# One exponent shift per query block instead of one per head pair, in an attention kernel

## The chip, the cores and the metric

The kernel runs on one core of one Trainium2 chip. The metric is the device time of one execution in microseconds (us), lower is better. The kernel before took 1887.35 us, the median of three runs (1886.14 to 1888.05).

## What is computed

A cross-attention layer with a residual, followed by a small recurrent (state-space) layer. `x` is 4096 x 512 (four sequences of 1024), the context is 3202 x 512, there are 8 heads of 64. All of it is fp32.

```python
def _mha(q_in, kv_in, W_qkv, b_qkv, W_o, b_o):
    ...
    q, k, v = (heads(q_in, Wq, bq), heads(kv_in, Wk, bk), heads(kv_in, Wv, bv))
    scores = jnp.einsum('bhqd,bhkd->bhqk', q, k) * (1.0 / np.sqrt(HD))
    attn = jax.nn.softmax(scores, axis=-1)
    out = jnp.einsum('bhqk,bhkd->bhqd', attn, v)
    ...
x = residual + _mha(_layernorm(x, g1, beta1), _layernorm(ctx, g1, beta1), ...)
xn = _layernorm(x, g2, beta2)
U = (xn @ W_in.T + b_in) @ Bmat
def step(s, u_t):
    s = jax.nn.silu(s @ A.T) + u_t
    return (s, s)
_, states = jax.lax.scan(step, ...)
x = x + states @ Cmat
return x + mod[:, None, :]
```

A softmax is the same whatever number is subtracted from all the scores of a row ahead of the exponential. The number need only keep the exponentials in range, so it may come from a sample of the keys.

## The kernel before

**Tiling.** The queries form 8 blocks Q of 512. The 3202 keys are 25 chunks of 128 and two left-over keys. The eight heads are four pairs hp; a pair fills 128 partitions, 64 for each head. A *unit* is one block and one head pair, with 25 key steps; block 7 is cut into halves (8 units of 13 steps). TensorE (PE) works on four pieces of 64x64 of its array at a time here, so that two heads and two halves of a chunk run beside each other.

**One step.** `scores` (PE, L1166) makes the scores of a chunk; `weights` (ScalarE, ACT, L1265) takes their exponential with the bias `shift`; `product` (PE, L1327) multiplies by the values; `add` (VectorE, DVE, L1273) adds the weights to `acc`, whose sum over partitions is the denominator. After the last step `fold`, `swap` (an ACT copy that exchanges the partition halves), `gather` (DVE), `sums` (PE) and `den` finish the unit.

**The shift.** Ahead of each unit (in block 7 of each first half), 32 times in all, a sample of 62 keys and the two left-over ones is scored: `sample` (PE, L1198, tile `sm` <- `q`, `kx`), `maximum` (DVE, L1212, L1213), `spread` (PE, L1220, a product that brings each partition's maximum to all of them), `base` (DVE, L1233, L1234, tile `shifts`). The left-over keys' weights come from the same scores: `extra` (ACT, L1240) takes their exponential, `rest` (two DVE operations on two rows, L1250) adds them to `acc`, and products with `vx` (L1316, L1340) add their values.

**Order.** Each engine runs its instructions in the order in which they are written, and waits for what the next one needs. The class `Plan` sets that order. Every piece of work has an engine, a cost, the pieces that it comes after, the buffers that it takes and gives, and a due time. `order()` plays the engines through time, and each free engine takes the ready piece with the earliest due time. The table `SHIFT` adds to the due time of each sort of piece its entry times a step of 2150 ns.

```python
due += self.SHIFT.get(sort, 0) * STEP
```

**Stages.** There are two plans. The first is the *lead* (`lead()`): context chunks c are loaded (`cx_c`), normalized (`xh_c`), turned by PE (`tp_c`, L347), copied to `ct`, and multiplied into keys and values. In the lead, chunks go in groups of four, g = 0 to 6. Group 0's values are plain products (`pv_c`, L619); groups 1 to 5 use seven products in place of eight on quarter tiles (L406): banks `pkx`, `pky`, `pvx`, `pvy` of a group take products of `ct_g`, of the sums `t5_g` and `t7_g` (made by DVE, L812) and of the weights' sums `sk5`, `sk7`, `sv5`, `sv7`. Joins (DVE, L602: `ks_2_22 <- pky_2` and so on) empty these banks. Of a group from 1 on, some chunks reach `ct_g` by DVE transposes (`pair_g`, L501) and 16 small transfers issued by SyncE (SP, L513). The last pieces of the lead are the query products of block 0 (`pq_0_hp`, L376), of which it has three. The second plan is the main one: all units, and between their steps the queries of the next block (seven products, L406, 128x128 tiles), the output projections and the recurrent part, whose last sweeps (L2051, L2125) form the tail. Both plans allow a buffer kind only as many open uses as its ring has.

## Time and profile before

| | |
|---|---|
| median of three runs | 1887.35 us |
| the profiled execution | 1886.87 us |
| its span, first to last instruction | 1885.1 us |
| TensorE busy in the span | 1871.5 us (99%) |
| VectorE busy | 1530.4 us (81%) |
| ScalarE busy | 1145.0 us (61%) |
| GpSimd (POOL) busy | 291.7 us (15%) |
| mean granted TensorE clock | 0.998 of full speed |

The profile comes from one execution. A row of its groups gives line, engine, operation, output tile <- input tiles, tile shape, number of records, then busy time in us and the mean ns of one record, then the idle time before and what ended it. One fp32 product leaves two records. A row of the timeline gives the start, the time from the first start to the last end of a run of like instructions (such runs overlap with the next), engine, line, operation and count; in brackets the idle time before it and what ended it. SPq and ACTq are the issuing of transfers by those engines. The lead ends at 195.3 us, and the tail begins at about 1780.

### The profile page before, as it was taken

To read this page: it belongs to the slowest core of one execution; us is meant where nothing else is said; L and a number is where in the kernel's file an instruction comes from. 1 tells how busy PE (TensorE), PEld (TensorE's weight loads), DVE (VectorE), ACT (ScalarE), POOL (GpSimd) and SP (SyncE) were. 2 spreads that over 40 slices of the span, in tenths; PEclk is the share of its full clock that TensorE was granted. 3 is DMA by queue.
4 is the path that set the end of the run, shared out by engine and by line. 5 is a ranking of instruction groups with operands and counts; after the bars stand their busy time and mean duration, and the time that the engine had idled before them with its cause. 6 is when DMAs were issued, how large, how long until landed. Compare 5 with 4: busy or idle time off the path is not lost.

```text
span 1885.1 us, 45215 instructions
## 1 busy us (share of the span) xinstructions
PE 1871.5 (99%) x18208; PEld 1027.5 (55%) x18208; DVE 1530.4 (81%) x1918; ACT 1145.0 (61%) x1439; POOL 291.7 (15%) x386
## 2 busy tenths in 40 slices
PE   9999999999999999999999999999999999999997
PEld 5887356545453535444454545353544545677674
DVE  6642689698888979798979888898979897998776
ACT  3242677565756567675656575657657565757653
POOL 6120300023000230023002200013002300101105
PEclk9999999999999999999999999999999999999999
DMA  8552242222333234313432233322431333435577
GB/s 256 162 168 88 63 121 75 90 65 80 107 98 105 68 86 122 100 45 93 109 107 68 76 104 99 106 68 88 125 93 44 91 102 92 151 105 162 158 200 233
DMA packets 260674, 206.04 MB, mean 109 GB/s; under 512 B 94633, under 2 KB 233897, under 8 KB 260461
## 3 DMA queue, kind: packets, MB, share of 16 engines
q1 hardware_dynamic: 256440, 196.48, 36.2%
q10 hardware_dynamic: 4020, 6.62, 1.2%
q8 instruction: 146, 2.39, 0.5%
q14 instruction: 68, 0.55, 0.1%
HBM read 156.32 MB, written 29.88 MB: 99 GB/s over the span
## 4 chain that ended last, share of the span: by engine, by line
PE 98%; DVE 1%; ACT 1%; DMA 0%; issue 0%; POOL 0%; SPq 0%; ACTq 0%; DVEq 0%; POOLq 0%
PE po L1327 33%; PE s L1166 32%; PE po L1352 5%; PE s L1179 4%; PE pax L406 3%; PE qx L406 3%; PE pay L406 2%; PE qy L406 2%; PE pkx L406 2%; PE pvx L406 2%; PE pvy L406 1%; PE pky L406 1%; PE pk L742 1%; PE pv L619 1%; PE sm L1198 1%; PE pu L1838 1%
## 5 line engine op out<-in xcount | busy, mean ns | idle before, releaser
L1265 ACT ACTIVATE p<-s,shifts 128x1024 f32<-128x1024 f32 x804 | 886.9, 1109 | 458.2 <-PE s L1166 336.4
L1273 DVE TENSOR_TENSOR acc<-p,acc 128x1024 f32<-128x1024 f32 (+1 forms) x732 | 894.8, 1225 | 119.0 <-ACT p L1265 90.8
L1327 PE MATMUL po<-p,v 64*64 64x512 f32 x5600 | 804.1, 590 | 0.0
L1166 PE MATMUL s<-q,k 64*64 64x512 f32 x5600 | 802.0, 589 | 0.0
L1166 PEld LDWEIGHTS s<-q,k 64*64 64x64 f32 x5600 | 263.6, 133 | 343.9 <-issue 291.2
L1327 PEld LDWEIGHTS po<-p,v 64*64 64x64 f32 x5600 | 264.7, 133 | 300.0 <-issue 260.1
L1725 POOL TENSOR_TENSOR xr<-xr,rowb 128x512 f32<-128x512 f32 x28 | 35.6, 1271 | 783.0 <-DVE acc L1273 570.5
L1439 DVE RECIPROCAL rd<-rd 128x256 f32<-128x256 f32 (+1 forms) x64 | 110.1, 1721 | 3.4 <-ACT rd L1434 3.1
L1179 PE MATMUL s<-q,k 64*64 64x256 f32 x1600 | 109.4, 378 | 0.2 <-ACT p L1265 0.2
L1352 PE MATMUL po<-p,v 64*64 64x256 f32 x1600 | 107.5, 377 | 0.0
L1820 POOL TENSOR_TENSOR xr<-x,modb 128x512 f32<-128x512 f32 x28 | 35.5, 1275 | 291.2 <-DVE acc L1273 238.3
L1179 PEld LDWEIGHTS s<-q,k 64*64 64x64 f32 x1600 | 67.3, 133 | 24.1 <-issue 4.9
L1352 PEld LDWEIGHTS po<-p,v 64*64 64x64 f32 x1600 | 67.8, 133 | 16.9 <-issue 0.5
L1296 ACT COPY swap<-acc 64x512 f32<-64x512 f32 (+1 forms) x70 | 40.2, 574 | 41.9 <-DVE acc L1273 40.2
L1212 DVE TENSOR_REDUCE m<-sm 128x1 f32<-128x256 f32 x64 | 24.0, 417 | 41.2 <-PE sm L1198 41.2
L1273 DVE TENSOR_TENSOR acc<-p,p 128x1024 f32<-128x1024 f32 x36 | 44.0, 1222 | 14.5 <-ACT p L1265 14.5
L1506 POOL TENSOR_SCALAR rstd_x<-mv_x 128x1 f32<-128x1 f32 x28 | 18.2, 648 | 231.3 <-DVE mv_x L1503 227.0
L602 DVE TENSOR_TENSOR ks<-pky,ks 128x512 f32<-128x512 f32 x15 | 10.4, 691 | 43.6 <-PE pky L406 22.2
L1301 DVE TENSOR_TENSOR acc<-swap,acc 64x512 f32<-64x512 f32 (+1 forms) x70 | 44.1, 630 | 1.5 <-ACT swap L1296 0.2
L1656 ACT ACTIVATE q<-qx,bias 128x256 f32<-128x256 f32 x42 | 17.6, 470 | 45.3 <-PE qx L406 45.3
L596 ACT ACTIVATE ks<-pkx,bias 128x256 f32<-128x256 f32 x40 | 16.8, 470 | 43.7 <-PE pkx L406 31.1
L1250 DVE TENSOR_TENSOR acc<-x,acc 2x512 f32<-2x512 f32 x56 | 38.0, 678 | 0.7
(321 smaller groups left out, 1849.0 us busy)
## 6 DMA issues: line engine op xcount, KB each, us to landing
k<-kd SPq DMA_DIRECT2D x432, 128.0 KB, 2.3
v<-vd SPq DMA_DIRECT2D x432, 128.0 KB, 2.4
xn<-x SPq DMA_DIRECT2D x448, 32.0 KB, 1.9
xr<-in_x_dram SPq DMA_DIRECT2D x30, 256.0 KB, 3.6
x1d<-xr SPq DMA_DIRECT2D x30, 256.0 KB, 3.1
x<-in_x_dram SPq DMA_DIRECT2D x28, 256.0 KB, 3.2
cx<-in_ctx_dram SPq DMA_DIRECT2D x25, 256.0 KB, 4.9
kd<-ks SPq DMA_DIRECT2D x20, 256.0 KB, 2.5
```

The source lines that it names most:

```text
L406: nc.tensor.matmul(to[:, b, :], still[:, i, b * P : (b + 1) * P], moving[:, i, :], start=(start and b == 0 and i == 0), stop=(i == 1), ski ...
L1166: nc.tensor.matmul(s[k0 : k0 + HD, a].rearrange("p b j -> p (b j)"), kts[(*w["at"][:2], c // 2)][r, b * CK + k0 : b * CK + k0 + HD], q[r], ...
L1179: nc.tensor.matmul(s[k0 : k0 + HD, a, b, :], kts[(*w["at"][:2], c)][r, b * CK + k0 : b * CK + k0 + HD], q[r], start=True, stop=True, skip_ ...
L1250: made = nc.vector.tensor_tensor(to[r], t[r], to[r], ALU.add)
L1265: nc.scalar.activation(t[:, :, :nb, :], w["ps"][c][:, :, :nb, :], AF.Exp, bias=w["shift"])
L1273: return nc.vector.tensor_tensor(w["acc"][:, :, :nb, :], t[:, :, :nb, :], before[:, :, :nb, :], ALU.add)
L1296: nc.scalar.copy(w["swap"][r], of[(1 - k) * HD : (2 - k) * HD])
L1301: made = nc.vector.tensor_tensor(of[r], w["swap"][r], of[r], ALU.add)
L1327: nc.tensor.matmul(w["po"][k][a * HD : (a + 1) * HD], vts[Q, hp, c // 2][r, c % 2, a * HD : (a + 1) * HD], t[r, a].rearrange("p b j -> p ( ...
L1352: nc.tensor.matmul(w["po"][k][a * HD : (a + 1) * HD, :QU], vts[Q, hp, c][r, b, a * HD : (a + 1) * HD], t[r, a, b, :], start=(c == 0 and b ...
L1439: nc.vector.reciprocal(w["rd"][:, part], (w["pd"] if last else w["rd"])[:, part])
L1725: return nc.gpsimd.tensor_tensor(xs[half][:, t], xs[half][:, t], rowb, ALU.add)
```

## The change

There is one sample for each block, eight in place of 32, and it covers all four head pairs with 32 keys each (30 and the two left-over ones). `sampled_by(Q)` writes it as seven pieces:

- `sample`: 16 products on 64x32 pieces of the array (32 keys, 256 queries), into two banks;
- `held` (ACT): the two banks are copied to an SBUF tile `ex`;
- `maximum` (DVE): one reduction of 128 x 1024 to 128 x 2;
- `sent`, `got` (SP): 128 x 2 numbers to DRAM, and 256 numbers back to all partitions;
- `base` (DVE): two reductions, then two small operations with the constant `marks`, which pick each partition's own bias for `extra`;
- `extra` (ACT): two exponentials of 512 columns, in place, for all left-over keys of the block.

The product `spread` is gone. A left-over key's weights are no longer added to `acc`: `rest` is one DVE operation on the copy that `swap` made, between `swap` and `gather`, with a column of `marks` that is 1 in the rows of the left-over keys and 0 elsewhere. The last unit still adds its two rows to `acc`. `vx` is written to four places by four transfers and a further one. The sample of block 0 and the fourth query product of block 0 are now in the lead (`FIRST` 3 to 4). All dates in `SHIFT` are new, and there are first-time dates for the pieces of the lead (`c.turn`, `v`, `k` and so on, which had 0).

```diff
-FIRST = 3
+FIRST = NC
+KS = 32
...
     SHIFT = {
-        "a": -10.5, "add": 549.25, "add.h": -100, "add.l": 237.5, "added": 96.5, "b": 3, "base": 11.5,
...
+        "a": 31.5, "add": 70, "add.h": 168, "add.l": -0.25, "added": 30.75, "b": 38, "base": 4.75,
...
+        "c.flip": 129, "c.load": -50.5, "c.move": -3.75, "c.scaled": -1.25, "c.stats": 4.75, "c.turn": -10.75,
...
+        "t": 218.25, "tied": 2.75, "v": 123.25, "wct": -62.25, "wk": -19.5, "wk.bias": -1.5, "wk.g": -64.75,
...
+    def sampled_by(Q):
+
+        v = {}
+
+        def sample():
+            v["s"] = s = [
+                m_tile([P, 512], f"sm_{Q}_{a}").rearrange("p (g j) -> p g j", g=2) for a in range(2)
+            ]
+            for g in range(2):
+                for t in range(2):
+                    for b in range(2):
+                        q = qt[Q, 2 * g + b]
...
+                        for a in range(2):
+                            r = slice(a * HD, (a + 1) * HD)
+                            nc.tensor.matmul(
+                                s[a][t * HD + b * KS : t * HD + (b + 1) * KS, g],
+                                kx[r, 2 * g + b, :],
+                                q[r, t],
...
+        def held():
...
+            for a in range(2):
+                nc.scalar.copy(t[:, a], v["s"][a])
+
+        def maximum():
+            v["m"] = small.tile([P, 2], F32, tag="m", name=f"m_{Q}", bufs=1)
+            nc.vector.tensor_reduce(v["m"], extras[Q].rearrange("p a g j -> p g a j"), AX.XY, ALU.max)
+
+        def sent():
+            nc.sync.dma_start(md[Q].rearrange("o (p g) -> (o p) g", g=2), v["m"])
+
+        def got():
+            v["all"] = small.tile([P, 2 * P], F32, tag="all", name=f"all_{Q}", bufs=1)
+            nc.sync.dma_start(v["all"], md[Q].to_broadcast([P, 2 * P]))
+
+        def base():
+            sh = shifts[:, Q * NC : (Q + 1) * NC].rearrange("p (g b) -> p g b", b=2)
+            of = v["all"].rearrange("p (t b k g) -> p g b t k", t=2, b=2, g=2)
+            for g in range(2):
+                nc.vector.tensor_reduce(sh[:, g], of[:, g], AX.XY, ALU.max, negate=True)
+            v["b"] = marks[:, 4:6]
+            nc.vector.tensor_scalar(v["b"], sh[:, :, 0], marks[:, 0:1], None, ALU.mult)
+            nc.vector.scalar_tensor_tensor(v["b"], sh[:, :, 1], marks[:, 1:2], v["b"], ALU.mult, ALU.add)
+
+        def extra():
+            for g in range(2):
+                t = extras[Q][:, :, g]
+                nc.scalar.activation(t, t, AF.Exp, bias=v["b"][:, g : g + 1])
...
+        if not w["last"]:
+            return nc.vector.scalar_tensor_tensor(
+                w["swap"], t, marks[:, 2 + b : 3 + b], w["swap"], ALU.mult, ALU.add
             )
...
-            plan.add(("sample", i), "PE", 440, partial(sample, w), q, d, ["m", "m"],
-                     [("q", of_q)], "quarters")
-            plan.add(("maximum", i), "DVE", 930, partial(maximum, w), [("sample", i)], d + 1000,
-                     ["max"])
-            plan.add(("spread", i), "PE", 130, partial(spread, w), [("maximum", i)], d + 1000, [],
-                     [], "quarters")
...
+        if Q and (hp, half) == (0, 0):
+            sample_pieces(plan.add, Q, [("sevenths.read", Q, k) for k in "2374"], max(s0 - REF, 0) * STEP,
+                          [("q", ("sevenths", Q, k)) for k in "15"])
...
-        head_pieces(plan, 0, range(FIRST, NC), first_xn, [("spread", 0)], -40 * STEP, 0, [("xn", "first")], "o")
```

The order of instructions moves at three places of the lead that the prediction speaks of. The first is TensorE at the start of the program, where `idle` is a run of products on zeros, `tp_c` the transposes of chunk c, and `pv_c` its values. Before:

```order
L1101 MATMUL idle_151<-a_t_91 128x128 x11
L347 MATMUL tp_c0_184<-ident_65,xh_c0_180 128x128 x4
L619 MATMUL pv_0_218<-wv_133,ct_0_183 128x512 x4
L347 MATMUL tp_c1_229<-ident_65,xh_c1_215 128x128 x4
L347 MATMUL tp_c2_236<-ident_65,xh_c2_212 128x128 x4
L619 MATMUL pv_1_248<-wv_133,ct_0_183 128x512 x4
L619 MATMUL pv_2_277<-wv_133,ct_0_183 128x512 x4
```

Now:

```order
L1215 MATMUL idle_156<-a_t_93 128x128 x11
L362 MATMUL tp_c0_189<-ident_66,xh_c0_185 128x128 x4
L362 MATMUL tp_c1_223<-ident_66,xh_c1_220 128x128 x4
L362 MATMUL tp_c2_230<-ident_66,xh_c2_217 128x128 x4
L716 MATMUL pv_0_238<-wv_138,ct_0_188 128x512 x4
L716 MATMUL pv_1_250<-wv_138,ct_0_188 128x512 x4
L362 MATMUL tp_c3_282<-ident_66,xh_c3_274 128x128 x4
```

The transposes of chunks 1 and 2 have moved ahead of the first values product `pv_0`.

The second is VectorE in the third group of the lead (g = 2 is being multiplied, g = 3 prepared). `L602` (now `L699`) are joins, `L310` and `L312` (now `L325`, `L327`) a chunk's statistics, `L501` (now `L598`) transposes for the small transfers, and `t5_3`, `t7_3` the sums of group 3's chunks. Before:

```order
L501 STREAM_TRANSPOSE pair_4_893<-xh_c16_891 128x16x32
L310 BN_STATS st_c19_907<-cx_19_808 128x6
L312 BN_AGGR mv_c19_909<-st_c19_907 128x2
L602 TENSOR_TENSOR ks_2_22_921<-pky_2_772,ks_2_22_921 128x512
L602 TENSOR_TENSOR vs_2_22_927<-pvy_2_796,vs_2_22_927 128x512
L1008 TENSOR_TENSOR rowb_88<-prr_925,rowb_88 128x512
L602 TENSOR_TENSOR ks_2_12_836<-pky_2_772,ks_2_12_836 128x512
L602 TENSOR_TENSOR vs_2_12_857<-pvy_2_796,vs_2_12_857 128x512
L602 TENSOR_TENSOR ks_3_11_975<-pky_3_978,ks_3_11_975 128x512
L550 COPY ct_3_844<-tp_c15_989 128x4x128
L812 TENSOR_TENSOR t5_3_1004<-ct_3_844 128x512
L812 TENSOR_TENSOR t5_3_1004<-ct_3_844,t5_3_1004 128x512
```

Now:

```order
L598 STREAM_TRANSPOSE pair_4_776<-xh_c17_879 128x16x32
L325 BN_STATS st_c22_930<-cx_22_763 128x6
L327 BN_AGGR mv_c22_932<-st_c22_930 128x2
L598 STREAM_TRANSPOSE pair_5_940<-xh_c20_934 128x16x32
L913 TENSOR_TENSOR t5_3_886<-ct_3_816,t5_3_886 128x512
L913 TENSOR_TENSOR t7_3_953<-ct_3_816 128x512
L325 BN_STATS st_c23_955<-cx_23_888 128x6
L327 BN_AGGR mv_c23_957<-st_c23_955 128x2
L913 TENSOR_TENSOR t7_3_953<-ct_3_816,t5_3_886 128x512
L699 TENSOR_TENSOR ks_2_22_963<-pky_2_842,ks_2_22_963 128x512
L699 TENSOR_TENSOR vs_2_22_972<-pvy_2_854,vs_2_22_972 128x512
```

The join `ks_2_22` stood ahead of both `t5_3` rows before; now the sums `t5_3` and `t7_3`, and the statistics of chunks 22 and 23, stand ahead of it.

The third is TensorE at the end of the lead, where the first scores `s_0_0_0_c` of the first unit follow. Before:

```order
L742 MATMUL pk_6_3_1565<-ct_6_1434,wk_132 128x130 x4
L376 MATMUL pq_0_1_1576<-xn_0_1137,wq_96 128x512 x4
L376 MATMUL pq_0_2_1586<-xn_0_1137,wq_96 128x512 x4
L1198 MATMUL sm_0_0_0_0_1632<-q_0_0_1521,kx_75 64x256
L1198 MATMUL sm_0_0_0_1_1633<-q_0_0_1521,kx_75 64x256
```

and, two scores and a maximum later,

```order
L1220 MATMUL sm_0_0_0_0_1632<-twice_72,m_0_0_0_1647 64x64
L1220 MATMUL sm_0_0_0_1_1633<-twice_72,m_0_0_0_1647 64x64
L376 MATMUL pq_o_1660<-xn_0_1137,wq_96 128x512 x4
L1166 MATMUL s_0_0_0_2_1681<-q_0_0_1521,k_0_0_0_1_393 64x512 x4
L1166 MATMUL s_0_0_0_3_1689<-q_0_0_1521,k_0_0_0_1_393 64x512 x4
```

Now (of the sample's 16 rows the last two):

```order
L426 MATMUL sm_0_0_1555<-q_0_2_1538,kx_76 32x256
L426 MATMUL sm_0_1_1556<-q_0_2_1538,kx_76 32x256
L503 MATMUL pky_5_1482<-ct_5_1232,sk7_524 128x256 x4
L503 MATMUL pvx_5_1474<-wv_138,t7_5_1349 128x256 x4
L503 MATMUL pvy_5_1489<-sv7_381,ct_5_1232 128x256 x4
L979 MATMUL pb_2_1603<-ones_71,shift_wv_467 128x1 x4
L716 MATMUL pv_24_1609<-wv_138,ct_6_1398 128x512 x4
L716 MATMUL pv_25_1628<-wv_138,ct_6_1398 2x512 x4
L1107 MATMUL prr_1633<-shift_rowv_1617,ones_71 128x512
L1107 MATMUL prm_1644<-wp_t_639,mean_1423 128x512
L1280 MATMUL s_0_0_0_0_1691<-q_0_0_1430,k_0_0_0_0_510 64x512 x4
L1280 MATMUL s_0_0_0_1_1696<-q_0_0_1430,k_0_0_0_0_510 64x512 x4
```

The sample stood right ahead of the first scores, with the spread and the fourth query product `pq_o` behind two of them. Now the sample of all four head pairs stands eight products ahead of the first scores, with the products `pq_0_3` and `pkx_5` ahead of it, and the spread and `pq_o` are gone from among the scores.

216 lines of the change are left out of this document (113 added, 103 removed).

## The prediction

> **What bounds the kernel now.** I read the page's totals first, then the table by stretches, then the groups of instructions on TensorE (PE), and last the timeline at the places that the change touches.
>
> ```profile
> span 1885.1 us, 45215 instructions
> PE 1871.5 (99%) x18208; PEld 1027.5 (55%) x18208; DVE 1530.4 (81%) x1918; ACT 1145.0 (61%) x1439; POOL 291.7 (15%) x386
> PE 98%; DVE 1%; ACT 1%; DMA 0%; issue 0%; POOL 0%; SPq 0%; ACTq 0%; DVEq 0%; POOLq 0%
> ...
> 0.00:195.30 195.30, 192.98 (x870) 147.61 (x870) 94.98 (x183) 66.99 (x121) 52.02 (x114) 1.00 0.57 168
> 195.30:1780.00 1584.70, 1584.70 (x15929) 812.83 (x15930) 1360.89 (x1598) 1028.36 (x1210) 212.65 (x240) 1.00 0.34 96
> 1780.00:1886.00 106.00, 93.80 (x1418) 67.03 (x1410) 74.57 (x138) 49.65 (x109) 27.00 (x33) 0.96 0.69 201
> ```
>
> The last three rows are the lead, the steady part and the tail (columns: window, its length, busy time of PE, weight loads, DVE, ACT, POOL, granted clock, DMA share, GB/s). In the steady part PE is busy for all of its 1584.70 us, and 98% of the chain of waits is PE. A microsecond of PE work more or less there is a microsecond of the end. What the change saves on DVE and ACT lies under PE: DVE has 224 us free in that stretch and ACT 556. So the sum is one of PE work, plus the places in the lead where the new order lets PE wait.
>
> **What PE loses.** The two groups that go, and where one of each stands among the steady work:
>
> ```profile
> L1198 PE MATMUL sm<-q,kx 64*64 64x256 f32 x256 | 19.8, 377 | 0.0
> L1220 PE MATMUL sm<-twice,m 64*64 64x64 f32 x256 | 12.4, 219 | 0.0
> ...
> 576.99 0.61 PE L1198 MATMUL sm<-q,kx 64*64 64x256 f32 x8
> 577.43 1.04 PE L1327 MATMUL po<-p,v 64*64 64x512 f32 x8
> 578.28 1.04 PE L1166 MATMUL s<-q,k 64*64 64x512 f32 x8
> 579.14 0.29 PE L1220 MATMUL sm<-twice,m 64*64 64x64 f32 x8
> 579.26 1.04 PE L1327 MATMUL po<-p,v 64*64 64x512 f32 x8
> ```
>
> The second column of the timeline is first start to last end, and groups overlap, so the price is start to start: 577.43 − 576.99 = 0.44 us for a sample and 579.26 − 579.14 = 0.12 for a spread. (The step of 512 columns between them takes 0.85, and a sample has half its columns: 0.43 is the better figure.) The groups have 256 records at 8 each, so 32 of each go: 32 × 0.55 = 17.6, or 17.9 by the rounded starts. I take **−17.7 us**. The fourth query product of block 0 only moves from the steady part to the lead; it costs the same there.
>
> **What PE gains: eight samples.** Each is 16 products of 256 columns on 64x32 pieces. No such piece is in this trace. The row above says that four 64x64 pieces of 256 columns, two records each, take 0.43 us together, two waves of 0.215. The nearest row with narrow pieces is the left-over keys' values, which the program runs on pieces of 128 rows and 32 columns:
>
> ```profile
> L619 PE MATMUL pv<-wv,ct 128*128 128x512 f32 x40 | 18.1, 598 | 0.8 <-ACT ct L550 0.8
> L619 PE MATMUL pv<-wv,ct 128*2 128x512 f32 x8 | 1.9, 592 | 0.0
> ```
>
> The first group has 40 records in 18.1 us, 3.6 for eight; eight of the narrow one take 1.9: two pieces beside each other in columns share the time. The order of the new loop gives eight products on eight different pieces, then eight more on the same ones. If all eight run at once, a sample is 2 × 2 waves of 0.215 = 0.86 us; if four at once, 1.73. I take 0.86, since both rows show that pieces that don't share rows and columns run together: **+6.9 us** (bounds +6.9 and +13.8). [...]
>
> **Changes of piece shape.** Seven samples stand among 64x64 work, two changes each. The trace has changes between 64x64 and the full array:
>
> ```profile
> 953.19 1.99 PE L406 MATMUL qx<-xn,wq 128*128 128x256 f32 x8
> 955.02 1.89 PE L406 MATMUL qy<-xn,wq 128*128 128x256 f32 x8
> ...
> 963.66 1.89 PE L406 MATMUL qx<-xn,wq 128*128 128x256 f32 x8
> 965.48 1.09 PE L1327 MATMUL po<-p,v 64*64 64x512 f32 x8
> ```
>
> The first full-array product takes 1.83 us to the next start, the last 1.82. Between their like the step is 1.73 (two rows of the lead, 86.73 and 88.46, shown below, have it). So a round trip is 0.2 us. Seven are 1.4; one of the other kind goes with the fourth query product, −0.2: **+1.2 us** (0 to 2.1, if what stands before the first pays as much again). [...]
>
> **The start of the lead.** The new order puts the transposes of chunks 1 and 2 ahead of the first values product pv_0; DVE, POOL and ACT do the same things in the same order until then.
>
> ```profile
> 6.22 0.81 PE L347 MATMUL tp_c<-ident,xh_c 128*128 128x128 f32 x4
> 7.50 3.70 PE L619 MATMUL pv<-wv,ct 128*128 128x512 f32 x8 [0.46 <-ACT ct L550]
> 9.90 0.73 DVE L534 TENSOR_SCALAR xh_c<-cx,mv_c,rstd_c 128x256 f32<-128x256 f32 x2
> 11.03 0.60 PE L347 MATMUL tp_c<-ident,xh_c 128*128 128x128 f32 x4
> 11.13 0.81 ACT L331 ACTIVATE xh_c<-cx,nmr_c,rstd_c 128x512 f32<-128x512 f32 x1 [3.41 <-POOL nmr_c L323]
> 12.00 0.65 PE L347 MATMUL tp_c<-ident,xh_c 128*128 128x128 f32 x4 [0.36 <-ACT xh_c L331]
> 12.49 7.06 PE L619 MATMUL pv<-wv,ct 128*128 128x512 f32 x16
> 20.72 3.70 PE L619 MATMUL pv<-wv,ct 128*128 128x512 f32 x8 [0.29 <-ACT ct L550]
> ```
>
> Chunk 1 is normalized only at 9.90 + 0.73 = 10.63, chunk 2 at 11.94. PE takes its work in order, so it stands still from 7.0 to 10.7, and the 3.53 us of pv_0 (7.50 to 11.03) come after 12.49 in place of before. Some 0.3 is given back, since the wait at 20.72 has then passed: **+3.2 us**. An idle PE may also lose its clock, as at the end of this run:
>
> ```profile
> 1872.73 0.32 PE L2051 MATMUL py_o<-scan,c 64*64 64x32 f32 x4 [1.66 <-ACT scan L2288]
> ...
> 1874.00:1877.00 3.00, 3.00 (x20) 1.03 (x12) 2.19 (x9) 0.90 (x3) 0.63 (x1) 0.50 0.85 275
> ```
>
> After the gap of 1.66 us the clock stood at 0.50 for about 3.4 us. In the lead, such a stretch from 11.0 to 14.4 would first cover the wait for chunk 2, and slow 2.5 us of work to half: **+1.2 us** (0 to 2.2).
>
> **The lead's third group.** In the new DVE order t5_3, t7_3 and the statistics of chunk 23 stand ahead of the join ks_2_22, which frees a bank for PE's product pky_2. In the order before, that join came first.
>
> ```profile
> 83.30 10.34 SPq L513 DMA_DIRECT2D ct<-pair  x16
> 81.08 1.47 SPq L610 DMA_DIRECT2D vd<-vs  x2
> cx<-in_ctx_dram SPq DMA_DIRECT2D x25, 256.0 KB, 4.9
> 86.73 1.89 PE L406 MATMUL pkx<-t,sk 128*128 128x256 f32 x8
> 88.46 1.89 PE L406 MATMUL pvx<-sv,t 128*128 128x256 f32 x8
> 89.53 0.69 DVE L602 TENSOR_TENSOR ks<-pky,ks 128x512 f32<-128x512 f32 x1 [2.62 <-ACT ks L596]
> ```
>
> Count from T, the end of the last product on ct_1. PE reaches pky_2 after eleven products of 1.73 and two transposes of 0.45: T + 19.9. SP may start the 16 moves of ct_3 at T (they overwrite ct_1): 10.3 us and two stores of 0.7, then six issues of about 0.5, then the load of chunk 23, which lands 4.9 later: T + 19.6. DVE then has the statistics (0.8), half of t7_3 (0.6) and the join (0.7): T + 21.7, and 0.3 to 0.7 for the hand-overs. PE waits **+2.5 us** (0 if the loads run ahead, 6 if the moves wait longer for SP).
>
> **The end of the lead.** Sample 0 is followed by some 13 us of other PE work (three products of 1.73, the values of two chunks at 3.5 and 1.9, small ones). Its chain is two copies, a maximum, two DMAs and the base; each step's nearest row is here:
>
> ```profile
> L592 ACT COPY vs<-pvx 128x512 f32<-128x512 f32 x20 | 11.7, 584 | 19.9 <-PE pvx L406 14.1 <-DMA vd<-vs 4.0 <-ACT ks L596 1.8
> L1212 DVE TENSOR_REDUCE m<-sm 128x1 f32<-128x256 f32 x64 | 24.0, 417 | 41.2 <-PE sm L1198 41.2
> ct<-pair SPq DMA_DIRECT2D x64, 32.0 KB, 1.9
> 197.77 3.70 PE L376 MATMUL pq_o<-xn,wq 128*128 128x512 f32 x8
> 198.60 2.12 ACT L1265 ACTIVATE p<-s,shifts 128x1024 f32<-128x1024 f32 x2 [2.46 <-DVE shifts L1234]
> ```
>
> Copies 2 × 0.58, maximum about 1.2 (1024 elements against 256 in 0.42), DMAs about 2 each, base about 1 behind three short jobs on DVE: 9 to 9.5 us, under the 13. So it stalls nothing; without that cover it would cost those 9. But the fourth query product, which covered the first weights before, is gone from there, and the third scores wait for a weights step: **+0.5**. In blocks 1 to 7 some 34 us of PE work lie between the sample and the first use; the same chain is hidden three times over. The left-over keys' add (two per unit at 0.68 on DVE before) becomes one, off PE.
>
> **Sum:** −17.7 + 6.9 + 1.2 + 3.2 + 1.2 + 2.5 + 0.5 = **−2.2 us**. The profiled execution took 1886.87 (1.77 outside its span), 0.48 under the median 1887.35. So 1884.7 profiled, and **1885.2** for the median. The tail's order hardly changes; ±1.
>
> **Rivals.**
> (a) The lead doesn't stall: its small waits take the place of others, the clock stays. Against it speaks that the first gap follows from the order alone. Without the third group's and the clock's terms the sum is −5.9; without the first one too, −9.1: 1878.2 to 1881.4. Chance 0.24.
> (b) Four pieces at once: a sample costs 1.73, the sum is −2.2 + 6.9 = +4.7, 1892.0, **slower**. It decides from 0.86 + 6.0 / 8 = 1.6 us a sample (3.8 us over before). For it speaks that no row shows more than four; against it the narrow row. Chance 0.13.
> (c) The chain through DRAM isn't ready at the lead's end: with loads' 4.9 us for each of the two DMAs it takes 15.3 us in place of 9.5, 2.3 over the cover: 1887.5. Chance 0.08.
> (d) The stalls at their full bounds (clock 2.2, third group 6): +4.5 on the forecast, 1889.7. Chance 0.08.
> The forecast itself: 0.47, with 1882.7 to 1887.7 as its own range.
>
> **How the numbers follow.** 0.2%, 3.8 us, is about what a measurement of this kernel can tell from no change. Faster is under 1883.6: all of (a) and a sixth of the forecast, 0.24 + 0.08 = 0.32. Slower is over 1891.1: most of (b) and a little of (d), 0.13. The same: 0.55. The range from 1879.5 to 1889.7 leaves out (b), half of (d) and a part of (a), in all 0.2 or so.
>
> **What would show it.** The sample's group with 16 x 2 records: 0.86 us start to start (right), 1.73 (b). A PE gap from 7.0 to 10.7 with a granted clock under 1 behind it; a wait of 1 to 4 us at a pky product near 95, put down to DVE's ks; sample 0's base ready before the first weights; the steady part still without a gap, some 10 us shorter from its first scores to the tail. What would make it wrong above all: a DVE order in the lead whose waits I followed at two places only, and more such places.

## The result and the profile after

The changed kernel took 1898.69 us (median of six runs, 1896.32 to 1901.1), the kernel before 1887.44 beside it (six runs). The ratio is 1.0059, with an interval of 1.0046 to 1.0072: **11 us slower**, where 2 us faster was forecast and 1889.7 was the upper end of the range. Run again the changed kernel took 1894.51 against 1887.39, a ratio of 1.0041 (1.0028 to 1.0053); a part of why its own time varies is found below, in place 5.

Totals and the chain of waits, from the page of the changed kernel (profiled execution 1901.1 us):

```profile
PE 1861.1 (98%) x17952; PEld 920.0 (48%) x17952; DVE 1492.1 (79%) x1731; ACT 1141.3 (60%) x1407; POOL 305.6 (16%) x395
PE 81%; DMA 3%; DVE 2%; ACT 2%; issue 1%; ACTq 0%; DVEq 0%; SPq 0%; POOLq 0%
```

TensorE's work did fall, from 1871.5 us to 1861.1. The chain of waits, which was 98% TensorE, is now 81%, with transfers, VectorE and ScalarE in it. Its shares add up to 89% only: the view follows the chain back no further than 215 us, so the lead is not in it. What was lost, and where, is read by three stretches: up to the first scores of block 0, from there to the first scores of block 7, and the rest. First the kernel before, then the changed one (columns as in the prediction):

```profile
0.00:195.80 195.80, 193.48 (x878) 147.97 (x882) 94.98 (x183) 67.33 (x122) 52.52 (x114) 1.00 0.57 168
195.80:1618.00 1422.20, 1422.20 (x13180) 693.91 (x13176) 1218.46 (x1409) 923.66 (x1069) 188.07 (x210) 1.00 0.31 89
1618.00:1886.00 268.00, 255.80 (x4158) 185.59 (x4150) 217.01 (x327) 154.00 (x250) 51.08 (x63) 0.98 0.60 175
```
```profile
0.00:216.10 216.10, 202.26 (x910) 152.00 (x910) 96.19 (x187) 70.69 (x127) 49.17 (x120) 0.97 0.50 148
216.10:1632.60 1416.50, 1404.57 (x12897) 588.86 (x12900) 1181.93 (x1243) 917.72 (x1036) 201.67 (x212) 1.00 0.33 91
1632.60:1900.00 267.40, 254.29 (x4150) 179.17 (x4142) 213.98 (x303) 152.88 (x245) 54.80 (x63) 0.99 0.60 175
```

The first stretch, which is the lead, is 20.3 us longer, the second 5.7 shorter, the last the same. In the lead TensorE is idle for 13.8 us in place of 2.3, and in the second stretch, where it never stood before, it is idle for 11.9. There are five places.

**1, the start.** TensorE in the changed kernel's timeline:

```profile
6.13 0.77 PE L362 MATMUL tp_c<-ident,xh_c 128*128 128x128 f32 x4 [0.20 <-DVE xh_c L631]
10.39 1.12 PE L362 MATMUL tp_c<-ident,xh_c 128*128 128x128 f32 x4 [3.49 <-DVE xh_c L631]
12.92 8.40 PE L716 MATMUL pv<-wv,ct 128*128 128x512 f32 x16
12.90:16.40 3.50, 3.50 (x7) 1.51 (x6) 3.15 (x10) 0.59 (x1) 2.65 (x8) 0.60 0.48 165
```

The gap is 3.49 us, with one of 0.51 before 12.02, and what follows runs slowly: a group of transposes takes 1.1 in place of 0.6, sixteen records of values products 8.40 in place of 7.06. In the last row, a stretch of the windows view, the granted clock is 0.60: it is 0.50 from 10.39 to 15.68, and 1.00 behind that.

**2, the lead's group 1.** ACT, SP and PE in the timeline of the changed kernel; `cb` is the second context of the problem, 3200 rows of 64 (800 KB), and `cb2` (second ACTq row) its last two rows (0.5 KB):

```profile
48.57 0.35 ACTq L1004 DMA_DIRECT2D cb<-in_ctxb_2048x_dram  x1
49.01 1.31 SPq L707 DMA_DIRECT2D vd<-vs  x2
50.42 8.02 SPq L610 DMA_DIRECT2D ct<-pair  x8
56.23 0.51 ACTq L1004 DMA_DIRECT2D cb<-in_ctxb_2048x_dram  x1
56.86 0.47 ACT L693 ACTIVATE ks<-pkx,bias 128x256 f32<-128x256 f32 x1 [6.53 <-DMA cb<-in_ctxb_2048x_dram]
57.79 3.75 PE L503 MATMUL pkx<-t,sk 128*128 128x256 f32 x8 [5.88 <-ACT ks L693]
57.70:61.20 3.50, 3.41 (x8) 2.53 (x8) 1.89 (x3) 0.00 (x0) 0.00 (x0) 0.50 0.77 167
```

ScalarE issues both loads. The second is issued only at 56.23, and ScalarE stands there for 6.53 us with a bank copy (`ks <- pkx`) behind it; TensorE waits 5.88 for that bank, and then runs at a clock of 0.50, until 63.47. In the kernel before, both loads were issued together, at another place and without a wait:

```profile
39.15 0.92 ACTq L903 DMA_DIRECT2D cb<-in_ctxb_2048x_dram  x2
```

The first of the two stores `vd <- vs` issued from 49.01 on ran beside the 800 KB of `cb` and landed at 56.20, and the issue of `cb2` follows at 56.23. (The row's releaser, `cb` itself, had landed at 55.91.) SyncE's next `ct` move stood 2.4 us, until 56.56, and its wait is put down to the second of these stores, which landed at 56.54, 6.8 us behind its issue. That `cb2` stood for the first store is read from these times; it was not tried by itself.

**3, the third group.** Two waits in TensorE's timeline, 2.55 us together, the first for a copy of ScalarE, the second for a join of VectorE:

```profile
101.27 1.99 PE L503 MATMUL pkx<-t,wk 128*128 128x256 f32 x8 [1.28 <-ACT ks L693]
104.53 1.78 PE L503 MATMUL pky<-ct,sk 128*128 128x256 f32 x7 [1.27 <-DVE ks L699]
```

**4, the first weights.** ACT, SP and PE at the lead's end:

```profile
213.22 1.33 ACT L467 ACTIVATE ex<-ex,marks 128x512 f32<-128x512 f32 x2 [6.35 <-DVE marks L462]
215.18 0.58 ACT L823 COPY vs<-pv 128x512 f32<-128x512 f32 x1
215.93 2.84 SPq L734 DMA_DIRECT2D vx<-second  x4
218.87 0.38 SPq L826 DMA_DIRECT2D vd<-vs  x1
221.45 2.12 ACT L1324 ACTIVATE p<-s,shifts 128x1024 f32<-128x1024 f32 x2 [5.69 <-issue]
221.65 1.26 POOL L1647 TENSOR_TENSOR sq<-wq 128x512 f32<-128x512 f32 x1 [45.23 <-DMA vd<-vs]
222.62 1.13 PE L1280 MATMUL s<-q,k 64*64 64x512 f32 x4 [4.52 <-ACT p L1324]
```

The base is ready by 213.2, so the chain through DRAM was in time: the sample's exponentials run then. But the first weights start only at 221.45. The main plan's tiles reuse the lead's memory, and the lead's last store (`vd <- vs` of chunk 24) was issued at 218.87, behind four `vx` transfers and behind a copy that ScalarE did after the exponentials, and landed 2.2 us later. GpSimd's first work of the main plan starts at the same time, and its wait is put down to that store. Behind TensorE's wait the clock is 0.50 until 227.31.

**5, behind the samples of blocks 1 to 7.** One of seven like this, TensorE's waits being 7.4 us together:

```profile
574.26 1.04 PE L1280 MATMUL s<-q,k 64*64 64x512 f32 x8
575.23 1.09 PE L426 MATMUL sm<-q,kx 64*32 64x256 f32 x32
576.25 1.09 PE L1280 MATMUL s<-q,k 64*64 64x512 f32 x8
578.96 0.32 SPq L449 DMA_DIRECT2D md<-m  x1
581.90 0.32 SPq L453 DMA_DIRECT2D all<-md  x1
587.12 0.48 DVE L459 TENSOR_REDUCE shifts<-all 128x2 f32<-128x128 f32 x2 [2.99 <-DMA all<-md]
588.22 1.33 ACT L467 ACTIVATE ex<-ex,marks 128x512 f32<-128x512 f32 x2 [1.91 <-DVE marks L462]
590.61 1.09 PE L1280 MATMUL s<-q,k 64*64 64x512 f32 x8 [1.25 <-ACT p L1324]
```

The store takes 2.9 us until the read can be issued, the read 5.2 until DVE has it. Sample to base are 12.9 us. The first use of the base by a score's weights is some 34 us away, but the left-over keys' own exponentials (588.22) stand in ScalarE's order only five weights behind the sample. ScalarE waits 1.91, the ring of scores fills up, and TensorE waits 1.25.

### The profile page after: what moved, and what is told of

It reads as the page before. It is cut to its first block, busy times and chain, and to the rows that moved or that the text cites. A ratio compares the mean times of both kernels' runs of the same rounds, so it can differ in the third digit from the quotient of the medians.

```text
span 1899.3 us, 44466 instructions
## 1 busy us (share of the span) xinstructions
PE 1861.1 (98%) x17952; PEld 920.0 (48%) x17952; DVE 1492.1 (79%) x1731; ACT 1141.3 (60%) x1407; POOL 305.6 (16%) x395
## 4 chain that ended last, share of the span: by engine, by line
PE 81%; DMA 3%; DVE 2%; ACT 2%; issue 1%; ACTq 0%; DVEq 0%; SPq 0%; POOLq 0%
PE s L1280 29%; PE po L1386 29%; PE po L1411 5%; PE s L1293 4%; PE qx L503 3%; PE pax L503 3%; PE pay L503 2%; PE qy L503 2%; DMA all<-md 2%; DMA md<-m 1%; ACT p L1324 1%; PE pd L1440 1%; DVE acc L1332 1%; PE pu L1900 1%; PE po L1375 1%
## 5 line engine op out<-in xcount | busy, mean ns | idle before, releaser
L1332 DVE TENSOR_TENSOR acc<-p,acc 128x1024 f32<-128x1024 f32 (+1 forms) x732 | 911.4, 1250 | 115.2 <-ACT p L1324 88.8
L1280 PE MATMUL s<-q,k 64*64 64x512 f32 x5600 | 724.2, 591 | 11.9 <-ACT p L1324 11.9
L1386 PE MATMUL po<-p,v 64*64 64x512 f32 x5600 | 722.3, 590 | 0.0
L1280 PEld LDWEIGHTS s<-q,k 64*64 64x64 f32 x5600 | 211.0, 133 | 401.3 <-issue 355.4
L1386 PEld LDWEIGHTS po<-p,v 64*64 64x64 f32 x5600 | 212.1, 133 | 355.9 <-issue 330.2
L1411 PE MATMUL po<-p,v 64*64 64x256 f32 x1600 | 112.2, 377 | 0.0
L1293 PEld LDWEIGHTS s<-q,k 64*64 64x64 f32 x1600 | 67.3, 133 | 25.5 <-issue 3.8
L1411 PEld LDWEIGHTS po<-p,v 64*64 64x64 f32 x1600 | 67.2, 133 | 21.3 <-issue 1.7
L1568 POOL TENSOR_SCALAR rstd_x<-mv_x 128x1 f32<-128x1 f32 x28 | 30.6, 1093 | 279.5 <-DVE mv_x L1565 277.8
L1576 ACT ACTIVATE xh_y<-x,nm_y,rstd_y 128x512 f32<-128x512 f32 x30 | 24.2, 807 | 83.5 <-POOL nm_y L1570 83.5
L699 DVE TENSOR_TENSOR ks<-pky,ks 128x512 f32<-128x512 f32 x15 | 10.4, 690 | 49.7 <-PE pky L503 30.7
L598 DVE STREAM_TRANSPOSE x<-xh_x 128x512 f32<-128x512 f32 x28 | 19.6, 704 | 15.2 <-ACT xh_x L1576 10.7
```

The lines of the kernel that those rows point to most:

```text
L1280: nc.tensor.matmul(s[k0 : k0 + HD, a].rearrange("p b j -> p (b j)"), kts[(*w["at"][:2], c // 2)][r, b * CK + k0 : b * CK + k0 + HD], q[r], ...
L1293: nc.tensor.matmul(s[k0 : k0 + HD, a, b, :], kts[(*w["at"][:2], c)][r, b * CK + k0 : b * CK + k0 + HD], q[r], start=True, stop=True, skip_ ...
L1332: return nc.vector.tensor_tensor(w["acc"][:, :, :nb, :], t[:, :, :nb, :], before[:, :, :nb, :], ALU.add)
L1386: nc.tensor.matmul(w["po"][k][a * HD : (a + 1) * HD], vts[Q, hp, c // 2][r, c % 2, a * HD : (a + 1) * HD], t[r, a].rearrange("p b j -> p ( ...
L1411: nc.tensor.matmul(w["po"][k][a * HD : (a + 1) * HD, :QU], vts[Q, hp, c][r, b, a * HD : (a + 1) * HD], t[r, a, b, :], start=(c == 0 and b ...
```

## The experiments

The theory after the result: the forecast PE terms hold, and the waits at the five places (with the half clock behind three of them) are the loss. The rival: the new work on TensorE, or the maxima's way through DRAM, is what costs. All edits are made in the changed kernel. From `e5` on, pieces are moved in the lead's finished order, by a list that names what is moved and behind what it is put:

```diff
-        for piece in plan.order():
+        pieces = plan.order()
+        place = lambda n: [p["name"] for p in pieces].index(n)
+        for what, behind in [...]:
+            piece = pieces.pop(place(what))
+            pieces.insert(place(behind) + 1 if behind else 0, piece)
+        for piece in pieces:
             piece["run"]()
```

**The dates of the lead alone.**

```diff
     SHIFT = {
...
-        "weights": 17.75, "yb": -25, "a.load": 176, "bu": 72.25, "c.copy": -73.25, "c.factors": 11,
...
+        "weights": 17.75, "yb": -25, "heads": 41.5, "q": -13.75,
```

> The changed kernel without its first-time dates for the lead's pieces (they are 0 again, as before); the main plan keeps its new dates. Theory 1 (the lead's new order costs most of the loss: gaps of 3.5, 5.9, 1.3 and 1.3 us on TensorE, half a clock behind two of them, some 16 us until the first scores): the first scores start 13 to 16 us earlier than in the changed kernel. Sample 0 now stands right ahead of them, so its chain of 11 us is uncovered there and 8 to 9 us come back as one gap; the first weights' wait of 4.5 us goes. In all 1884 to 1890. Theory 2 (the new sample and its chain in the steady blocks cost it): the steady part is unchanged, so 1896 to 1899.

Measured: 1888.29 us, ratio 1.0002 (0.9993 to 1.0012). The first scores come at 203.47 in place of 216.16, 12.7 us earlier, just under what was expected. The gaps of places 1 to 3 are gone (two others of 0.8 have come, at 124.7 and 198.9), and a chain that is no longer covered takes the place of the fourth, in TensorE's timeline:

```profile
203.47 1.95 PE L1269 MATMUL s<-q,k 64*64 64x512 f32 x16 [1.71 <-ACT vs L812]
214.39 1.98 PE L1269 MATMUL s<-q,k 64*64 64x512 f32 x8 [8.97 <-ACT p L1313]
```

So the new dates of the lead make places 1 to 3, and what they bought is also seen: with the old dates block 0's chain is not covered, and costs 9 us, as much as the prediction named for that case.

**The start.** `("v", 0)` goes first in the lead's order.

```diff
-        for piece in plan.order():
+        for piece in sorted(plan.order(), key=lambda p: p["name"] != ("v", 0)):
```

> The changed kernel with the first values product pv_0 back ahead of the transposes of chunks 1 and 2, nothing else. Theory 1: the gap of 3.5 us at 6.9 goes, and the half clock behind it, so 4 to 5 us less, 1893.7 to 1894.7. Rival: the work behind it waits for loads or copies anyway, and takes back what is gained: 0 to 2 us less.

Measured: 1890.20 us, ratio 1.0013 (1.0003 to 1.0022), under the expected range: place 5's waits happen to be 3.4 us here in place of 7.4. The gap is gone, the first scores come 5.2 us earlier (210.94), and the window behind it has its clock back:

```profile
12.90:16.40 3.50, 3.50 (x11) 1.54 (x11) 3.22 (x9) 1.89 (x3) 2.30 (x7) 1.00 0.79 257
```

The order alone made the gap, and with the gap the low clock went (1.00 in this stretch, 0.60 in the changed kernel). Of the 5.2 us, 2.9 are gaps (3.49 and 0.51 less the 0.7 and 0.4 that are left); the rest goes with the clock.

**The second transfer counted.** The planner counts no landing time between two pieces of one queue: 5.6 us for the store and the read, which took 2.9 + 5.2 above. With an added piece for the landing it counts both:

```diff
-            before = [(name, Q)]
+            before = [add(("landed", Q), "IN", 0, lambda: None, [(name, Q)], d + 1000 * i)] and [] or [("landed", Q)] if name == "sent" and Q else [(name, Q)]
```

> The changed kernel, with the planner told that in blocks 1 to 7 the second transfer of the maxima starts only when the first has landed; this puts the exponentials of the left-over keys (and the base) three or four weights later on ScalarE and VectorE, and changes nothing on TensorE but the names that follow. Theory 1: the waits of TensorE of 0.6 to 1.4 us at the first steps of seven blocks (7.4 us in sum) come from ScalarE standing behind those exponentials; they go, 6 to 7.5 us less, 1891 to 1893. Rival: they come from the sample's own cost or shape change on TensorE: no change, 1897 to 1900.

Measured: 1891.16 us, ratio 1.0016 (1.0006 to 1.0026). Five of the seven waits are gone, and two of 0.18 and 0.17 are left; the scores' group waits for 4.5 us in place of 11.9, 4.14 of it at the first weights:

```profile
L1280 PE MATMUL s<-q,k 64*64 64x512 f32 x5600 | 724.6, 591 | 4.5 <-ACT p L1324 4.5
```

The way through DRAM is no shorter (at the sample shown above, 3.8 us from the store's issue to the read's, 2.9 before). The exponentials now stand eight weights behind the sample, not five, and the base has moved on VectorE with them. So it was the place of the chain's end, and not the way through DRAM by itself, that cost. The edit does not part the two engines; that it was ScalarE is read from the rows above, where the exponentials wait and the next weights stand behind them.

**The last values earlier.** A first edit for place 4, by the date of the last two values products:

```diff
-            v, u = {}, used(c)
+            v, u = {}, used(c) - (123.25 * STEP if c >= n_g * GC else 0)
```

> The changed kernel with the values of the last two chunks (pv_24, pv_25) some 30 us earlier in the lead, so that their stores and the four transfers of vx are done before the first weights. Theory 1: the wait of 4.5 us before the third scores, and the half clock behind it, come from the last store of the lead, whose memory the first weights take; they go. But sample 0 then has only some 8 us of TensorE work behind it for a chain of 11, so 1 to 3 us come back: 3 to 5 us less in all, 1894 to 1896. Rival: the first weights wait for the left-over keys' chain or the bias: no change or worse.

Measured: 1897.34 us (four runs), ratio 1.0049 (1.0033 to 1.0066), outside what was expected. The wait for the first weights falls to 1.25 (at 221.13), but a new one opens ahead of it:

```profile
218.78 1.09 PE L1107 MATMUL prr<-shift_rowv,ones 128*128 128x512 f32 x2 [2.69 <-DVE shift_rowv L593]
```

`shift_rowv` stands on DVE behind the base; without the last values products in front, TensorE gets there too early.

**The loads of `cb` earlier.** List: `('d.cb', 'd.win'), ('d.cb2', 'd.cb')`.

> The changed kernel with the two loads of the second context (cb, 800 KB, and cb2, its last two rows) issued by ScalarE right behind the load of win, some 12 us earlier, nothing else. Theory 1: the gap of 5.9 us at 57.8 comes from the issue of cb2, which stands 6.7 us on ScalarE until an earlier transfer lands, with the key copies behind it; the 800 KB run beside group 2's small transfers. Loaded earlier the gap goes, and the half clock behind it: 5 to 7.5 us less, 1891 to 1894. Rival: the earlier place only shifts the same wait to the loads of chunks ahead of it: 0 to 2 us less, with a gap at another place of the lead.

Measured: 1891.97 us, ratio 1.0023 (1.0013 to 1.0033). The gap of 5.88 us is gone, and with it the third group's is 0.34 in place of 2.55, though nothing was moved there. A new one of 3.1 stands at 75.1, on a join behind statistics that wait for a context chunk (`cx`). This is a third place of the kind that the prediction followed in the third group.

**The last stores earlier.** The last values product (`pv_25`) and its copy are put earlier, and block 0's exponentials and chunk 24's store right behind chunk 24's copy. List: `(('v', 25), 'wv.pb'), (('v.copy', 25), ('rowv', 2)), (('extra', 0), ('v.copy', 24)), (('v.store', 24), ('v.copy', 24))`.

> The changed kernel with the left-over keys' values (pv_25) ahead of pv_24 on TensorE, their copy and the copy of chunk 24's values ahead of the left-over keys' exponentials on ScalarE, and so their five transfers 3 us earlier; the work behind sample 0 stays the same. Theory 1: the first weights wait for the last of these transfers (4.5 us before the third scores): 3 to 5 us less, 1893.5 to 1896. Rival (the first weights wait for the bias or the exponentials): no change.

Measured: 1891.04 us, ratio 1.0013 (1.0004 to 1.0023), under the expected range; place 5's waits are 4.1 here. The last store is issued at 214.84 in place of 218.87, and the wait is nearly gone:

```profile
214.84 0.38 SPq L826 DMA_DIRECT2D vd<-vs  x1
218.58 1.09 PE L1285 MATMUL s<-q,k 64*64 64x512 f32 x8 [0.67 <-ACT p L1329]
```

**The third group's sums behind the joins.** List: `t5_3`, `t6_3`, `t7_3`, `t4_3` behind the joins `ks_2_22` and `vs_2_22`.

> The changed kernel with group 3's four sums (t5_3, t7_3) behind the joins ks_2_22 and vs_2_22 on VectorE, as the order before had them, nothing else. Theory 1: the two gaps of 1.3 us at 101 and 104.5 go, 2 to 3 us less, 1895.5 to 1897, and the trace has no gap over 0.3 us between 62 and 200. Rival: the sums are then late for group 3's products, and as much comes back some 10 us later.

Measured: 1894.67 us (five runs), ratio 1.0036 (1.0022 to 1.005), a little under the expected range. But only one of the two waits is gone, the other became 2.09. The timeline shows its chain:

```profile
101.30 0.69 DVE L325 BATCH_NORM_STATS2 st_c<-cx 128x6 f32<-128x512 f32 x1 [4.22 <-DMA cx<-in_ctx_dram]
102.95 1.99 PE L503 MATMUL pky<-ct,sk 128*128 128x256 f32 x8 [2.09 <-DVE ks L699]
```

It is the prediction's chain link for link: chunk 23 is loaded behind the moves, its statistics wait on DVE, the join waits behind them, TensorE behind the join. The sums alone were not the cause; in the changed kernel they and the load hold up the join together.

**Five together** (`e2`, `e3`, `e5`, `e7`, `e8`).

> The changed kernel with all five at once: pv_0 first, cb's loads earlier, the sums behind the joins, the last stores earlier, and the second transfer of the maxima counted by the planner. If the five waits are separate and the new sample itself costs TensorE what the trace shows (1.02 us and 0.11 before it), the gains add: 5 + 6 + 2.5 + 4 + 7.5 = 25 less than the changed kernel, 1872 to 1877, which is 10 to 15 faster than before. If the waits hide one another, 1878 to 1886. If it stays over 1887 the new sample costs more than it saves.

Measured: 1875.09 us (four runs), ratio 0.993 (0.9913 to 0.9946), **faster than before** by 12.6. Behind 13 us one wait of the lead is left, in the third group, the same chain:

```profile
91.38 2.03 PE L503 MATMUL pky<-ct,sk 128*128 128x256 f32 x4 [3.39 <-DVE ks L699]
```

**The statistics too.** To the list come `c.stats` and `c.factors` of chunk 23, behind the third group's sums.

> The five together, and also the statistics of chunk 23 behind the joins. In the five together one gap of 3.4 us is left at 91.4: the join ks_2_22 stands on VectorE behind the statistics of chunk 23, whose load SyncE issues only after group 3's 16 small transfers (the prediction's chain for this place, which the sums alone did not decide). Theory 1: the gap goes, 3 to 4 us less than the five together, 1871 to 1873. Rival: chunk 23 is then late for its own transpose and the gap comes back later in the lead: 1874 to 1876.

Measured: 1875.06 us (1869.52 to 1876.84, six runs), ratio 0.9923 (0.9909 to 0.9937), no better than the one before, and the figure of the rival, though not at its place, which was later in the lead. The gap at 91.4 is gone, and one of 3.78 stands at 70, as in the `cb` experiment:

```profile
68.38 0.69 DVE L325 BATCH_NORM_STATS2 st_c<-cx 128x6 f32<-128x512 f32 x1 [6.95 <-DMA cx<-in_ctx_dram]
70.08 3.37 PE L503 MATMUL pvy<-sv,ct 128*128 128x256 f32 x8 [3.78 <-DVE vs L699]
```

Four of its runs took about 1875 and two about 1869.6, so this wait probably depends on when the load of `cx` lands, for which VectorE waits 6.95 us in the first row; that is a guess, and only one of the slower ones has a trace.

**Chunk 19 too.** `c.stats` and `c.factors` of chunk 19 go behind the joins of group 1.

> As the run with chunk 23's statistics behind the joins, and chunk 19's statistics behind the joins of group 1 as well. In that run four of six executions took 1875 us and two 1869.6; the profiled one (1875.2) has a gap of 3.8 us at 70.1, where the join vs_1_22 stands on VectorE behind the statistics of chunk 19, which wait 7 us for their load beside the 1 MB load of wo. Theory 1: the gap goes in every execution: 1869 to 1872, and no wait over 1 us is left in the lead after 13. Rival: the slow load then holds up another piece (the transposes by VectorE, group 2's sums): 1873 to 1876.

Measured: 1870.79 us (five runs) against 1888.19, **ratio 0.9908** (0.9894 to 0.9922): 17.4 us faster than the kernel before. From its page:

```profile
PE 1852.5 (99%) x17952; PEld 919.4 (49%) x17952; DVE 1492.0 (80%) x1731; ACT 1142.1 (61%) x1407; POOL 306.6 (16%) x395
PE 97%; DVE 1%; DMA 1%; ACT 0%; issue 0%; SPq 0%; POOL 0%; ACTq 0%; DVEq 0%; POOLq 0%
...
0.00:199.40 199.40, 196.70 (x910) 148.97 (x910) 95.74 (x187) 70.61 (x127) 49.94 (x120) 1.00 0.55 161
199.40:1601.50 1402.10, 1401.44 (x12897) 591.18 (x12900) 1182.23 (x1242) 918.40 (x1037) 201.81 (x212) 1.00 0.33 91
1601.50:1869.00 267.50, 254.41 (x4150) 179.23 (x4142) 214.06 (x303) 153.09 (x245) 54.89 (x63) 0.99 0.62 175
```

(the last three rows are its windows). All work of the changed kernel is still there, in the same number of products. The lead is 3.6 us longer than before, which is the moved query product; the chain of waits is TensorE again.

**The sample's order.** In the kernel with the statistics moved, each pair of products in a row goes to one piece, in place of eight pieces in turn:

```diff
-            for g in range(2):
-                for t in range(2):
-                    for b in range(2):
...
+            for t in range(2):
+                for b in range(2):
+                    for a in range(2):
+                        for g in range(2):
```

> As the run before, but the 16 products of a sample are written so that each two in a row go to the same 64x32 piece (the loop over the pair of head pairs is innermost), in place of eight different pieces and then the same eight. If the array runs whatever fits, a sample stays at 1.02 us; if products start in the written order and a second one on a piece waits for the first, pieces beside each other idle: from 1.3 us (half the overlap lost) to 3.5 us (no overlap but inside a pair), in the steady part TensorE's own time, 7 times.

Measured, one execution: 1875.84 us. A sample takes 1.08 us start to start (556.63 to 557.71) against 1.02, and all eight are busy for 9.2 us against 8.8, so the order of the pieces hardly matters.

**The changed kernel again**, as it is.

> The changed kernel once more, unchanged, so that it has times beside the two below. If its waits at block starts vary with how fast the maxima's transfers land, their sum differs from the 7.4 us of the first profile (the four variants, which don't touch them, show 4 to 5.4) and the time is within 1896 to 1901.

Measured: 1894.51 us, a little under the expected range. Its block waits are 2.9 us in place of 7.4; the lead's are 3.56, 5.37, 2.60 and 4.64. This is why the variants above are read by their waits: a median near 1890 may hold 4 us of them. What makes these waits longer in one execution than in another is not known.

TensorE's waits in the profiled executions, in us (start: the longest one between 6.5 and 13 us):

| | start | `cb` | third group | first weights | blocks 1 to 7 |
|---|---|---|---|---|---|
| changed kernel | 3.49 | 5.88 | 2.55 | 4.52 | 7.4 |
| the same again | 3.56 | 5.37 | 2.60 | 4.64 | 2.9 |
| start mended | 0.72 | 5.82 | 2.85 | 4.15 | 3.4 |
| second transfer counted | 3.60 | 5.73 | 2.99 | 4.14 | 0.35 |
| last values earlier | 3.48 | 5.26 | 2.74 | 1.25 (2.69 ahead of it) | 5.4 |
| `cb` earlier | 3.90 | 0 (3.1 at 75) | 0.34 | 4.43 | 4.3 |
| last stores earlier | 3.58 | 5.91 | 2.51 | 0.67 | 4.1 |
| sums behind the joins | 3.17 | 5.10 | 2.09 | 4.11 | 3.5 |
| five together | 0.46 | 0 | 3.39 | 0.66 | 0 |
| statistics too | 0.46 | 0 (3.78 at 70) | 0 | 0.65 | 0 |
| chunk 19 too | 0.46 | 0 | 0 | 0.66 | 0 |

## Why the prediction was wrong, step by step

The rows of the changed kernel's first profile against those of the version without the waits account for nearly all of the 30.8 us between them (1901.1 and 1870.33). Places 1 to 3 are 3.1 + 5.9 + 2.55 = 11.6 of gaps (3.1 since 0.46 and 0.40 are left of the first). For the clock the author's estimate is half of TensorE's busy time at 0.50, by the eight records that take 3.75 us there (57.79) and 1.99 at 1.00 (101.27): 2.4 behind the first place (10.39 to 15.68, less a wait of 0.51), 2.8 behind the second (57.79 to 63.47) and 2.3 behind the fourth (222.62 to 227.31). Place 4 is 3.9 of gap, place 5 is 7.4. That makes 30.4.

| step of the prediction | forecast | found |
|---|---|---|
| old samples and spreads, each pair | 0.55 | 0.55 at 16 unit starts, 0.82 to 1.12 at 12 |
| eight samples and their changes of shape | +6.9 and +1.2 | +9.0 (1.13 each) |
| start of the lead | +3.2 | +3.1 |
| clock behind it | +1.2 | +2.4 |
| third group | +2.5 | +2.55, half of it another wait |
| lead's group 1 (`cb`) | not followed | +5.9, and 2.8 of clock |
| end of the lead | +0.5, "it stalls nothing" | +4.5, and 2.3 of clock |
| blocks 1 to 7 | 0, "hidden three times over" | +2.9 to +7.4 |
| all PE work saved less added, first scores of block 0 to those of block 7 | 11.7 with the moved product | 20.1 |

**What held.** The eight pieces run at once: 32 records in 1.02 us, not 1.73, so rival (b) is out. From the product before (574.26) to the product behind (576.25) are 1.99, of which the product takes 0.86: a sample costs 1.13 with both changes, where 1.06 was summed. The start came as worked out, and `e2` shows it by its own cause. The clock behind it fell as forecast, but stayed at 0.50 until 5.3 us behind the gap, where a stretch of 3.4 had been reckoned: 2.4 us in place of 1.2, over the bound of 2.2. The third group's total agrees partly by luck: 1.28 of the 2.55 is a wait at a `pkx` product for ScalarE's copy, which the prediction had not, and in `e5` all but 0.34 went without an edit there. The chain that it had followed is there all the same: `e8` shows it alone, and `e9` takes it away. The chain at the lead's end took 11.6 us, not 9 to 9.5 (sample at 201.51, base ready at 213.12), under a cover of 13: rival (c) did not come, and (a), a lead without stalls, was wrong. Rival (d) put higher prices on the stalls that were seen; the loss came from those that were not.

**What failed, 1: "it stalls nothing".** The step followed the base, which was in time, and not the other thing that the first weights need: the lead's memory, whose last store landed at 221.1, 0.4 us ahead of the first weights. The prediction had named the fourth query product as cover that goes, and put 0.5 on it; it was 4.5, and `e7` takes all but 0.67 of it away by issuing that store 4 us earlier.

**What failed, 2: "the same chain is hidden three times over".** 34 us of TensorE's work do lie between sample and first use. But part of the chain's end is queued on an engine that works in order. The cover that counts is the one on ScalarE, from the sample to the place of the left-over keys' exponentials: five weights, shorter than the chain. `e3` shows it: the same way through DRAM, the chain's end placed three weights later, and 0.35 of wait in place of 7.4.

**What failed, 3: the lead was followed at two places.** The last sentence of the prediction named this as the thing that would make it wrong. The third place, the loads of `cb`, was the dearest single wait: its new date moved an issue on ScalarE to where it stood 6.53 us until an earlier store had landed, with a bank copy behind it; `e5` moves the two loads and the wait is gone.

**What was undersized: the gain.** From the first scores of block 0 to those of block 7 the version without waits is 1422.2 − 1402.1 = 20.1 us shorter. By the prediction's prices it would be 28 samples and spreads at 0.55, less seven new samples at 1.06, and the moved product at 3.65 (8 records of 0.43 and a change of shape): 15.4 − 7.4 + 3.65 = 11.7. Of the 8.4 more, 1.7 only went elsewhere: the groups by shape show that 32 records of the recurrent part (`pu`, 64x128) and 8 records of values now lie behind the border, and the last stretch, which lost three samples and spreads, did not get shorter for that.

The largest part is the price of the old samples and spreads, which the prediction took from one place. There (576.14 to 580.12) four products, a sample and a spread take 3.98 us, 0.55 more than four steps of 0.8585. Counted in the same way, it is 0.55 at 16 of the 28 unit starts, but 0.82 to 0.85 at six and 1.11 or 1.12 at another six; at one of these, seven products, a sample and a spread take 6.85 us (905.29 to 912.14), 0.84 more than seven steps. Together that is 20.4 in place of 15.4. At the first six of these the array pieces fall out of step, and the next full-array product starts later too, by 0.36 us in the block shown here. It is seen in TensorE's timeline of the kernel before, and of the changed one:

```profile
951.87 1.39 PE L1166 MATMUL s<-q,k 64*64 64x512 f32 x8
```
```profile
556.24 1.04 PE L1280 MATMUL s<-q,k 64*64 64x512 f32 x8
557.20 1.99 PE L503 MATMUL qx<-xn,wq 128*128 128x256 f32 x8
```

In the kernel before, the eight records of this product were spread over 1.39 us: one starts at 951.87 and the next three at 952.23, 0.36 us apart, so its four array pieces had fallen out of step. The full-array product at 953.19 (shown in the prediction) comes 1.32 us behind the last 64x64 product, in the changed kernel 0.96. Six of the seven blocks have 1.3 there and one 1.21, together 2.4 us. Of 1242 rows with eight records of 512 columns in that stretch, 246 were over 1.2 us from first start to last end; in the version without waits none of 1293 was over 1.1. In the block shown the step falls apart behind an old sample (at 907.87), and stays so until the full-array product. 1.7, 5.0 and 2.4, less 0.5 for the new samples (1.13 each, not 1.06), make 8.6, where 8.4 were to be found. Why twelve unit starts cost more than the other sixteen was not tried.

## What to carry to other kernels

Cover for a long chain has to be counted on every in-order engine on which a piece of the chain is queued, not only on the engine that sets the end: here the 34 us on TensorE left 7.4 us of waits, and three weights more on ScalarE took all but 0.35 of them away. In a new order, each load's issue and each piece of work on freshly loaded data that stands ahead of a bank's join can pass the transfer's delay on to TensorE, as here by 5.88 us (`cb2`), 3.39 (chunk 23) and 3.78 (chunk 19); so every such place is to be walked through, and the last stores of a stage whose memory is reused with them. A planner that omits one landing time doesn't save it: the wait turned up on other engines here, 1.91 us on ScalarE and 1.25 on TensorE in the block shown.

## What the runs showed of the hardware that was not expected

- Eight pieces of 64x32 do run together: eight records start within 0.06 us of 575.23, and the 32 records of 256 columns take 1.02 us with their change of shape, 1.08 in another order of the pieces.
- The way of a kilobyte through DRAM to all partitions is long, in the DMA rows of the changed kernel's page (KB each, median us from issue to landing):

```profile
all<-md SPq DMA_DIRECT2D x8, 128.0 KB, 4.5
md<-m SPq DMA_DIRECT2D x8, 1.0 KB, 2.8
```

The prediction took 2 us for each by the 32 KB moves (1.9); measured were 2.8 and 4.5. It is not the size alone: the 128 KB loads of `k` and `v`, also issued by SyncE, took 2.6 in the same profile.
- Three long waits of TensorE cost more than their length: behind gaps of 3.5, 5.9 and 4.5 us the granted clock was 0.50 for another 5.3, 5.7 and 4.7 us. Behind the two of 1.3 in the third group it stayed at 1.00 (101.00 to 106.50), and behind the 2.09 of `e8` eight records took 1.99 us, as they do at 1.00 (at 0.50 they took 3.75). The prediction reckoned from a 0.50 behind 1.66 us, so the length of the wait alone does not tell.
- Array pieces that had fallen out of step, one of them 0.36 us ahead of the other three, stayed so, in the block shown, until the next full-array product, which then came 1.32 us behind the last 64x64 product, 0.36 later than behind pieces in step (0.96).
- A transfer's issue seems to have waited for an earlier transfer whose data it does not use: ScalarE stood 6.5 us with the issue of `cb2`, 0.5 KB, which came 0.03 us behind the landing of a store of SyncE.
